# A cross-attention kernel: another order for the first five blocks, with division behind the values and seven-product matmuls from block 0

## The chip, the cores and the metric

The kernel runs on one core of one Trainium2 chip. The metric is the device time of one execution in microseconds (us), which is the time of that core. The core has five engines that matter here: TensorE (PE in the profile, its weight loads PEld), VectorE (DVE), ScalarE (ACT), GpSimd (POOL), and SyncE (SP), which here only issues DMAs. Each engine takes its own instructions in the order in which they were written; an instruction that must wait for another engine holds up everything behind it on its own engine. SBUF is the memory on the chip, PSUM the accumulator that TensorE writes to.

## What is computed

All in float32, with 16 batches of 1024 rows and 512 features, a context of 64 rows for each batch, and 16 heads of 32 features:

```python
def _ada_ln(x, c, W_ss, b_ss):
    h = (x - mu) / jnp.sqrt(var + EPS)          # mean and variance of each row
    scale, bias = jnp.split(jax.nn.silu(c) @ W_ss + b_ss, 2, axis=-1)
    return (1.0 + scale)[:, None, :] * h + bias[:, None, :]
xq = _ada_ln(x, cond, Wss_q, bss_q)
xkv = _ada_ln(ctx, cond, Wss_kv, bss_kv)
q = xq @ Wq + bq
k, v = split(xkv @ Wkv + bkv)
attn = softmax(q k^T / sqrt(32))                # for each head, over the 64 context rows
out = x + ((attn @ v) @ Wp + bp)
```

## The kernel before

**Tiling.** The 16384 rows are cut into 32 blocks of 512 (`i`; `NB` is 32, `TB` 512), two for each batch. Features are in four groups of 128 (`c`), rows of a block in four tiles of 128 (`t`), the 64 context rows in two halves of 32 (`z`). Keys and values are made for two batches at a time (`keys` or `key_products` with `key_tiles`, `value_products` with `value_tiles`).

**One block** goes through these steps, each a function:
- `load_x` (L139, SP) brings in 512 rows, 1 MB. `q_stats` (L296, VectorE) takes mean and variance of each row; `q_scale` (L305) makes the factors, in `rstd_of` (L263): with `apart` on ScalarE and POOL, without it on ScalarE and VectorE. `hidden` (L325, ScalarE) normalises.
- `turn` (L490, VectorE) transposes 32x32 pieces into `ht`; `move` (L502) puts them in their places in `xt` with 16 DMAs of 64 KB, all from SP. Features are then across partitions. (Block 0 is turned on TensorE instead.)
- The query projection has two forms. The plain form (`queries`, L533, with `queried` on ScalarE to copy out and add the bias) uses weights that were scaled for the batch (`query_weights`, L480) and 16 matmuls of 128x512 a block. The seven-product form (`query_product`, L607, with `query_out`, `query_added`, `query_seed`) multiplies halves and sums of halves by Strassen's scheme, 28 matmuls of 128x256 in place of 32 such; it needs `scale_features` (L562, ScalarE), `query_weight_sums` once and `feature_sums` (L593, both POOL).
- `scores` (L666) makes two PSUM pairs for each `z`; VectorE takes maxima out of them (`maximum`), ScalarE copies them to SBUF (`copied`). With `crossed` the two engines begin at different pairs, without it both begin at the first. `maxima` (L721) combines and spreads the maxima over the tile, `subtract` (L727, POOL unless told otherwise) takes them off, `weights` (L733, ScalarE) exponentiates.
- The division by the sum has two forms. Ahead of the values: `sums`, `inverse` and a `spread` on VectorE, then `divide` (L757, POOL) of both weight tiles, then `mix` (L809, TensorE) and `mixed` (ScalarE) to copy out. Behind the values: `total` (L765, POOL) adds the halves, `row_total` and `inverse_rows` (VectorE, five small DMAs through DRAM), `spread_rows`, and after `mix` the copy out is itself the division, `divided` (L800, VectorE).
- The output projection has two forms as well. Plain: `project` (L849), four times 4 matmuls of 128x512, with `projected`, which adds to the residual tile, on VectorE; `residual` (L330, POOL) has added the bias to that tile. Seven products: `biased` (ScalarE) seeds the PSUM bank with the bias, `row_sums` (L903, POOL) makes sums of halves, `product` (L915) multiplies, `added` (L942, VectorE) adds to the residual tile, seven times a block; `weight_sums` (L876, POOL) is done once.

**Order.** The order on every engine is written out by hand, as the sequence of calls at the end of the function: a way in for blocks 0 to 3, a regular loop from block 4 to 29 in which the steps of neighbouring blocks are interleaved, and a way out for the last two. Before, block 0 and 1 divide ahead of the values and are projected plainly, block 2 divides ahead of the values and is projected with seven products, and blocks 0 to 4 make their queries plainly. From block 3 on it divides behind the values, from block 5 on queries have seven products.

```python
        vb_tiles[i] = spread(i, v, f"vb_{i}", other=i in (1, NB - 1))
...
    mix(0, apart=False)
    mixed(0)
```

**Buffers.** A tile with the tag of an older one in a pool of one or two buffers waits until the older one is no longer read. `x` has two, `r` (residuals) two, `ht` one, `xt` two, `wq` two (also the sums of the query weights and features), `vb`, `qt`, `ot`, `s1` one each, `big0` to `big3` one each (first the scale and shift weights, later the score tiles: `i % 2 * 2 + z`). In PSUM, `ps_s` has two pairs of banks for scores and for `mix`, and four single banks go round in `ring`, of which two are left (`ring[:] = [0, 1]`) once banks 2 and 3 accumulate the seven products.

Of the kernel before, what the change touches and what calls it, by code (L numbers as in the profile page):

```python
# [20 lines left out]
def cross_attention_block(  # L21
# [16 lines left out]
):  # L38

# [99 lines left out]
    def load_x(i):  # L139
        t = xpool.tile([P, NT, H], F32, tag="x", name=f"x_{i}")  # L140
        nc.sync.dma_start(t, rows_of(x, i))
        x_tiles[i] = t
# [34 lines left out]
    for c in range(NC):  # L177
        nc.sync.dma_start(
            b_v_sb[c * 32 : (c + 1) * 32, :],
            b_kv[H + c * P : H + (c + 1) * P].rearrange("(o h) -> o h", o=1).to_broadcast([32, P]),  # L180
        )
# [123 lines left out]
    def q_scale(i, kvb=None):  # L305
        n = NT if kvb is None else NT + 1
        q_rstd[i] = rstd_of(q_mv.pop(i)[:, :n, :], n, "q", i > 1)
        if kvb is not None:
            kv_rstd[kvb] = (q_rstd[i], NT)
# [170 lines left out]
    def query_weights(b):  # L480
        t = qpool.tile([P, NC, H], F32, tag="wq", name=f"wq_{b}")
        for c in range(NC):
            scale = ss["q"][:, c, b : b + 1]
            if b == 0 and c % 2:
                nc.vector.tensor_scalar_mul(t[:, c, :], w_q_sb[:, c, :], scale)
            else:
                nc.scalar.mul(t[:, c, :], w_q_sb[:, c, :], scale)
        wq_tiles[b] = t

    def turn(i, ts):  # L490

        if ts[0] == 0:
            ht_tiles[i] = hpool.tile([P, 4, NC, NT, 32], F32, tag="ht", name=f"ht_{i}")
        for t in ts:
            nc.vector.transpose(
                ht_tiles[i][:, :, :, t, :].rearrange("p k c b -> p c k b"),
                x_tiles[i][:, t, :].rearrange("p (c k b) -> p c k b", c=NC, k=4),
            )
        if ts[-1] == NT - 1:
            x_tiles.pop(i)  # L500

    def move(i):  # L502
# [3 lines left out]
        for k in range(4):  # L506
            for g in range(4):
                nc.sync.dma_start(  # L508
# [24 lines left out]
    def queries(i, o, later=False):  # L533
        xt, b = xt_tiles[i], i // BPB
        w = wq_tiles.get(b, w_q_sb)
        if o == 0:

            tag = "vb" if i in (1, 3) else "qt"
            qt_tiles[i] = qpool.tile([P, NC, TB], F32, tag=tag, name=f"qt_{i}", bufs=1)
# [13 lines left out]
    def queried(i, o):  # L553
        pq, b = pq_tiles.pop((i, o)), i // BPB
        dst = qt_tiles[i][:, o, :]
# [194 lines left out]
    def inverse(i):  # L750

        v = small.tile([P, HPC * NJ], F32, tag="v", name=f"v_{i}")
        both(v, l_tiles.pop(i), ALU.add)
        nc.vector.reciprocal(v, v)
        vb_tiles[i] = spread(i, v, f"vb_{i}", other=i in (1, NB - 1))
# [9 lines left out]
    def total(i):  # L765

        t = big.tile([P, HPC, TB], F32, tag=f"big{(i + 1) % 2 * 2}", name=f"sum_{i}")
# [3 lines left out]
    def row_total(i):  # L771
# [7 lines left out]
        )  # L779

# [187 lines left out]
    query_bias_rows()  # L968
    kv_stats(0)
# [10 lines left out]
    load_x(2)  # L980
    load_residual(0)
    load_projection_bias()
# [3 lines left out]
    move(1)  # L986
    load_projection()
    load_x(3)
# [8 lines left out]
    hidden(2, range(NT))  # L997


    scores(0, 0)  # L1000
    turn(2, range(NT))
    move(2)
    load_context(2)
    load_x(4)
    load_residual(1)
    residual(0)
    value_products(0)
    scores(0, 1)
    maxima(0)
    subtract(0, nc.vector, (0,))  # L1010
    value_tiles(0)
    subtract(0, nc.vector, (1,))
    queries(1, 0)
    query_weights(1)
    queries(1, 1)
    weights(0, 0)
    queries(1, 2)
    weights(0, 1)
    sums(0, 0)
    queries(1, 3)  # L1020
    query_weight_sums()
    sums(0, 1)
    inverse(0)
    divide(0)
    scores(1, 0)
    queries(2, 0)
    q_stats(3)
    queries(2, 1)
    q_scale(3)
    scores(1, 1)  # L1030
    maxima(1)
    subtract(1)
    queries(2, 2)
    hidden(3, (0, 1))
    mix(0, apart=False)
    mixed(0)
    hidden(3, (2, 3))
    queries(2, 3)
    turn(3, range(NT))
    move(3)  # L1040
    kv_stats(2)
    q_stats(4)
    project(0, 0)
    weights(1, 0)
    sums(1, 0)
    project(0, 1)
    weights(1, 1)
    residual(1)


    load_x(5)
    q_scale(4)
    kv_scale(2)
    scores(2, 0)
    sums(1, 1)
    inverse(1)
    divide(1)
    project(0, 2)
    context_hidden(2)
    hidden(4, (0, 1))  # L1060
    scores(2, 1)
    maxima(2)
    subtract(2)
    weight_sums()
    hidden(4, (2, 3))
    project(0, 3)
    queries(3, 0)
    queries(3, 1)
    queries(3, 2)
    turn(4, range(NT))  # L1070
    load_residual(2)
    move(4)
    mix(1)
    mixed(1)
    q_stats(5)
    weights(2, 0)
    queries(3, 3)
    project(1, 0)
    sums(2, 0)
    weights(2, 1)  # L1080
    project(1, 1)
    sums(2, 1)
    inverse(2)
    divide(2)
    q_scale(5)
    context_features(2)
    scale_features(4)
    project(1, 2)


    load_x(6)
    scores(3, 0, crossed=True)
    project(1, 3)
    ring[:] = [0, 1]
# [3 lines left out]
    queries(4, 0)  # L1098
    load_residual(3)
    hidden(5, (0, 1))  # L1100
    biased(2, 2)
    mix(2)
    mixed(2)
    hidden(5, (2, 3))
    q_stats(6)
    turn(5, range(NT))
    move(5)
    q_scale(6)
    row_sums(2, 0)
    load_x(7)  # L1110
    queries(4, 1)
# [3 lines left out]
    weights(3, 0)  # L1115
    added(2, 2)
    biased(2, 3)
    weights(3, 1)
    total(3)
    queries(4, 2)  # L1120
    keys(2)
    hidden(6, range(NT))
    scale_features(5)
    row_sums(2, 1)
    turn(6, range(NT))
    load_x(8)
    product(2, 7)
    q_stats(7)
    value_products(2)
    value_tiles(2)  # L1130
    row_total(3)
    inverse_rows(3)
    queries(4, 3)
    feature_sums(5)
# [199 lines left out]
```

## Time and profile before

| | us |
|---|---|
| median of 3 runs | 1058.74 (1057.19 to 1059.29) |
| the profiled execution | 1058.86 |
| its span, first to last instruction | 1057.1 |
| POOL busy with divide (L760), mean of one | 4.52 |
| POOL `subtract` (L729), mean of one of 58 | 4.56 |
| POOL `total` (L768), mean of one | 4.54 |
| VectorE `divided` (L805), mean of one of two a block | 1.22 |
| VectorE `row_total` (L773), mean of one | 2.28 |
| mean granted TensorE clock | 0.998 |

The profile is of one execution. A row of a group gives line, engine, operation, output and inputs by the program's names, their shapes, the count, then the busy time of all and the mean of one in ns, and the idle time of the engine just before them with what ended it. A row of the timeline gives start and length in us, engine, line, operation, and in brackets the idle time ahead of it. TensorE's rows are pipelined: the distance between starts, not the length, is what a stage costs. A row of the table by stretch gives the stretch, its length, then the busy time of PE, PEld, DVE, ACT and POOL with counts, the granted clock, the DMA share and GB/s.

In the way in, the first scores begin at 39.7 us, the scores of blocks 1, 2, 3 at 60.7, 89.6 and 125.9, those of block 4, with which the loop begins, at 162.0, and those of block 5 at 197.0.

### The profile page before, as it was taken

Reading aid. Unit: us, or ns where it says so; the run is one execution under the profiler, and the core shown is the slowest. Engines: PE = TensorE matmul, PEld = TensorE weight load, DVE = VectorE, ACT = ScalarE, POOL = GpSimd, SP = SyncE. Lnnn points to the kernel's source line nnn. Section 1 sums busy time; section 2 is a strip of 40 time slices with the busy share of each in tenths; the row PEclk is TensorE's granted clock in tenths of the full one; section 3 lists DMA queues with packets and bytes.
Section 4 is the critical chain, followed back from the end, with each engine's and each line's share of the span. In section 5 each row is a group of like instructions: output and inputs, shape, how many; then the busy total and the mean of one; then the engine's idle time right before and its main releaser. Section 6 shows DMA issues by size and latency. Waiting matters only on the chain.

```text
span 1057.1 us, 22537 instructions
## 1 busy us (share of the span) xinstructions
PE 1033.6 (98%) x8914; PEld 733.7 (69%) x8914; DVE 854.7 (81%) x1134; ACT 618.0 (58%) x951; POOL 752.7 (71%) x470
## 2 busy tenths in 40 slices
PE   6999998999999999999999999999999999999998
PEld 4534365777777787777787787777777777777433
DVE  5698648987789877888878878898778887776993
ACT  3566665665575655667556666566566765565330
POOL 0258794889768869788668986688886886787340
PEclk9999999999999999999999999999999999999999
DMA  9743444444535344544345443444454443334202
GB/s 337 248 127 111 130 122 127 155 150 147 161 94 162 123 140 145 171 148 127 106 131 164 153 158 112 126 141 150 139 157 134 152 134 116 98 115 162 82 30 90
DMA packets 99976, 147.27 MB, mean 139 GB/s; under 512 B 29944, under 2 KB 30096, under 8 KB 99872
## 3 DMA queue, kind: packets, MB, share of 16 engines
q1 hardware_dynamic: 99872, 145.85, 43.5%
q8 instruction: 70, 1.15, 0.5%
q14 instruction: 34, 0.28, 0.1%
HBM read 78.85 MB, written 34.44 MB: 107 GB/s over the span
## 4 chain that ended last, share of the span: by engine, by line
PE 80%; DVE 5%; POOL 5%; DMA 4%; SPq 2%; issue 2%; ACT 1%; POOLq 0%; DVEq 0%; ACTq 0%
PE pp L933 28%; PE pq L625 27%; PE po L825 6%; PE ps L673 6%; PE pp L852 5%; PE pq L542 3%; SPq L508 2%; PE pv L431 2%; PE pk L395 2%; POOL s L760 2%; DMA wss_kv<-in_L_xcond_Wss_kv_dram 2%; DMA b_p_sb<-in_L_xcond_bp_dram 1%; POOL s L729 1%; DMA x<-in_x_dram 1%; DVE s L729 1%
## 5 line engine op out<-in xcount | busy, mean ns | idle before, releaser
L729 POOL TENSOR_TENSOR s<-s,mb 128x2048 f32<-128x2048 f32 x58 | 263.1, 4560 | 160.8 <-DVE mb L716 160.8
L694 ACT COPY s<-ps 128x1024 f32<-128x1024 f32 x128 | 129.5, 1012 | 119.7 <-DVE m L685 82.9
L685 DVE TRANSPOSE_TENSOR_REDUCE m<-ps 128x32 f32<-128x1024 f32 x128 | 150.6, 1214 | 27.1 <-PE ps L673 27.1
L655 ACT ACTIVATE qt<-pq,bias_t 128x256 f32<-128x256 f32 x208 | 85.8, 463 | 110.9 <-PE pq L625 110.9
L933 PE MATMUL pp<-w_p_sb,ot 128*128 128x256 f32 x648 | 148.7, 379 | 0.0
L735 ACT ACTIVATE s<-s 128x2048 f32<-128x2048 f32 x64 | 122.3, 1911 | 42.4 <-POOL s L729 31.8
L947 DVE TENSOR_TENSOR r<-pp,r 128x512 f32<-128x512 f32 x189 | 122.5, 670 | 25.5 <-PE pp L933 19.8
L933 PEld LDWEIGHTS pp<-w_p_sb,ot 128*128 128x128 f32 x648 | 123.4, 190 | 17.4 <-issue 0.7
L768 POOL TENSOR_TENSOR sum<-s,s 128x2048 f32<-128x2048 f32 x27 | 122.7, 4543 | 0.8 <-ACT s L735 0.8
L933 PEld LDWEIGHTS pp<-WT,s 128*128 128x128 f32 x432 | 78.9, 192 | 54.0 <-issue 29.3
L933 PE MATMUL pp<-WT,s 128*128 128x256 f32 x432 | 109.3, 397 | 0.0
L933 PE MATMUL pp<-WT,ot 128*128 128x256 f32 x432 | 102.2, 380 | 0.0
L625 PE MATMUL pq<-xt_sums,wq_sums 128*128 128x256 f32 x416 | 101.0, 386 | 0.0
L321 ACT ACTIVATE x<-x,rstdq 128x512 f32<-128x512 f32 x128 | 96.7, 807 | 4.8 <-POOL rstdq L285 3.2
L625 PE MATMUL pq<-xt,wq_sums 128*128 128x256 f32 x416 | 99.0, 381 | 0.0
L625 PEld LDWEIGHTS pq<-xt_sums,wq_sums 128*128 128x128 f32 x416 | 77.0, 190 | 31.1 <-issue 21.8
L625 PE MATMUL pq<-xt,w_q_sb 128*128 128x256 f32 x416 | 98.4, 380 | 0.1
L260 DVE BATCH_NORM_STATS2 bs<-x 128x6 f32<-128x512 f32 x128 | 86.9, 679 | 5.0 <-DMA x<-in_x_dram 5.0
L662 DVE TENSOR_TENSOR qt<-pq,qt 128x256 f32<-128x256 f32 x104 | 39.1, 418 | 63.1 <-PE pq L625 62.5
L933 PEld LDWEIGHTS pp<-WT,ot 128*128 128x128 f32 x432 | 82.2, 190 | 11.0
L565 ACT ACTIVATE xt<-xt,ss_q 128x512 f32<-128x512 f32 x112 | 84.7, 810 | 6.1 <-DMA xt<-ht 4.3
L625 PEld LDWEIGHTS pq<-xt,w_q_sb 128*128 128x128 f32 x416 | 79.1, 190 | 11.0 <-PE pp L933 0.4
(139 smaller groups left out, 1725.0 us busy)
## 6 DMA issues: line engine op xcount, KB each, us to landing
x<-in_x_dram SPq DMA_DIRECT2D x32, 1024.0 KB, 6.4
r<-in_x_dram SPq DMA_DIRECT2D x32, 1024.0 KB, 5.5
xt<-ht SPq DMA_DIRECT2D x496, 64.0 KB, 2.0
out_dram<-r SPq DMA_DIRECT2D x54, 512.0 KB, 3.8
out_dram<-r SPq DMA_DIRECT2D x20, 256.0 KB, 2.0
wss_q<-in_L_xcond_Wss_q_dram SPq DMA_DIRECT2D x2, 1024.0 KB, 8.8
ctx<-in_ctx_dram SPq DMA_DIRECT2D x8, 256.0 KB, 3.2
wss_kv<-in_L_xcond_Wss_kv_dram SPq DMA_DIRECT2D x2, 1024.0 KB
```

The lines of the kernel that those rows point to most:

```text
L260: nc.vector.bn_stats(bs, r)
L321: nc.scalar.activation(dst, src, AF.Identity, bias=rstd[:, 1, j : j + 1], scale=rstd[:, 0, j : j + 1])
L565: nc.scalar.activation(xt[:, :, c, :], xt[:, :, c, :], AF.Identity, scale=ss["q"][:, c, b : b + 1], bias=ss["q"][:, NC + c, b : b + 1],)
L625: nc.tensor.matmul(qa[k][:, m * HT : (m + 1) * HT].rearrange("p (g n) -> p g n", g=2), lhsT=a[:, c, m * P : (m + 1) * P], rhs=x[:, :, c, : ...
L655: nc.scalar.activation(dst, src, AF.Identity, bias=bq_t[:, o : o + 1])
L685: nc.vector.tensor_reduce(m_tiles[i][:, z, 2 * e : 2 * e + 2, :], pss[e].rearrange("p r (j a) -> p r j a", a=32), AX.X, ALU.max, apply_tra ...
L694: nc.scalar.copy(s_sb[:, 2 * e : 2 * e + 2, :], pss[e])
L729: eng.tensor_tensor(s_tiles[i, z], s_tiles[i, z], mb_tiles[i], ALU.subtract)
L735: nc.scalar.activation(p, p, AF.Exp, scale=SCALE)
L768: nc.gpsimd.tensor_tensor(t, s_tiles[i, 0], s_tiles[i, 1], ALU.add)
L933: nc.tensor.matmul(acc[k][:, t * HO : (t + 1) * HO], lhsT=rows[:, c, t * P : (t + 1) * P], rhs=cols[:, c, :], start=n == 2 and t == 0 and ...
L947: nc.vector.tensor_add(r, acc[k].rearrange("p (t h) -> p t h", t=2), r)
```

## The change

The way in is written anew; loop and way out are the same. In words:
- blocks 0, 1 and 2 divide behind the values and are projected with seven products; block 4 makes its queries with seven products. `residual`, `inverse`, `divide`, `mixed` and `project` are gone from the way in. Block 1 gets its sums from two `sums` and the new `halves_total` on VectorE, blocks 0 and 2 from `total` on POOL;
- in `move`, for blocks 1, 2, 3 and 5, every second group of four DMAs is issued by POOL (8 of 16);
- the scaled weights of batch 1 are made by POOL in one instruction, not by ScalarE in four;
- `q_scale(2)` is done without `apart`;
- other places: x_3 in a buffer of `r`, `ht` of block 2 in `big2`, the sum of block 0 in `ot`, the queries of block 3 in `qt`, and a query tile is only taken when the first copy into it is written;
- `load_x(2)` ahead of the value bias, the residual and projection-bias loads later; statistics, turns, copies, exponentials and POOL's sums in another order.

```diff
-        t = xpool.tile([P, NT, H], F32, tag="x", name=f"x_{i}")
+        t = xpool.tile([P, NT, H], F32, tag="r" if i == 3 else "x", name=f"x_{i}")
...
-        q_rstd[i] = rstd_of(q_mv.pop(i)[:, :n, :], n, "q", i > 1)
+        q_rstd[i] = rstd_of(q_mv.pop(i)[:, :n, :], n, "q", i > 2)
...
+        if b:
+            scale = ss["q"][:, :NC, b : b + 1].to_broadcast([P, NC, H])
+            nc.gpsimd.tensor_tensor(t, w_q_sb, scale, ALU.mult)
...
-            ht_tiles[i] = hpool.tile([P, 4, NC, NT, 32], F32, tag="ht", name=f"ht_{i}")
+            pool, tag = (big, "big2") if i == 2 else (hpool, "ht")
+            ht_tiles[i] = pool.tile([P, 4, NC, NT, 32], F32, tag=tag, name=f"ht_{i}")
...
-                nc.sync.dma_start(
+                (nc.gpsimd if i in (1, 2, 3, 5) and k % 2 else nc.sync).dma_start(
...
+            tag = "vb" if i == 1 else "qt"
+            qt_tiles[i] = qpool.tile([P, NC, TB], F32, tag=tag, name=f"qt_{i}", bufs=1)
...
+        if i == 0:
+            t = opool.tile([P, HPC, TB], F32, tag="ot", name="sum_0")
...
+    def halves_total(i):
+        lt_tiles[i] = small.tile([P, HPC, NJ], F32, tag="lt", name=f"lt_{i}")
+        both(lt_tiles[i].rearrange("p r j -> p (r j)"), l_tiles.pop(i), ALU.add)
```

The new order from the keys of block 0 to the loop, the loads of the residuals left out, a line for each stretch:

```python
keys(0); hidden(2, range(NT)); turn(2, range(NT)); move(2); query_weights(1); load_x(4); value_products(0); value_tiles(0)
scores(0, 0, crossed=True); q_stats(3); queries(1, 0); q_scale(3); scores(0, 1); maxima(0); subtract(0, nc.vector)
queries(1, 1); hidden(3, range(NT)); weight_sums(); queries(1, 2); weights(0, 0); turn(3, range(NT)); queries(1, 3); weights(0, 1); total(0); move(3)
scores(1, 0, crossed=True); queries(2, 0); row_total(0); inverse_rows(0); load_x(5); scores(1, 1); maxima(1); subtract(1)
queries(2, 1); queries(2, 2); biased(0, 2); mix(0); spread_rows(0); divided(0); queries(2, 3); weights(1, 0); queries(3, 0, later=True)
row_sums(0, 0); q_stats(4, (0, 1)); sums(1, 0); q_stats(4, (2, 3), kvb=2); weights(1, 1); product(0, 1); added(0, 1); product(0, 2); row_sums(0, 1); q_scale(4, kvb=2); query_weight_sums()
scores(2, 0, crossed=True); added(0, 2); biased(0, 3); queries(3, 1, later=True); scores(2, 1); queried(3, 0); queried(3, 1); hidden(4, range(NT)); maxima(2); subtract(2)
product(0, 7); added(0, 7); product(0, 6); added(0, 6); queries(3, 2); sums(1, 1); halves_total(1); inverse_rows(1); product(0, 5); added(0, 5); turn(4, range(NT)); move(4); load_x(6)
product(0, 4); added(0, 4); product(0, 3); added(0, 3); weights(2, 0); biased(1, 2); weights(2, 1); total(2); mix(1); spread_rows(1); divided(1); context_hidden(2); queries(3, 3)
q_stats(5); q_scale(5); row_sums(1, 0); context_features(2); product(1, 1); added(1, 1); product(1, 2); added(1, 2); row_sums(1, 1); biased(1, 3); row_total(2); inverse_rows(2); scale_features(4)
scores(3, 0, crossed=True); feature_sums(4); product(1, 7); product(1, 6); added(1, 7); added(1, 6); scores(3, 1); maxima(3); subtract(3); query_product(4, 1); query_seed(4); hidden(5, (0, 1, 2))
product(1, 5); added(1, 5); query_product(4, 2); query_out(4, 2); product(1, 4); product(1, 3); hidden(5, (3,)); spread_rows(2); q_stats(6, (0, 1)); added(1, 4); added(1, 3); biased(2, 2)
mix(2); q_stats(6, (2, 3)); divided(2); turn(5, range(NT)); load_x(7); q_scale(6); row_sums(2, 0); move(5); query_product(4, 6); weights(3, 0); query_out(4, 6); product(2, 1); added(2, 1); product(2, 2); added(2, 2); weights(3, 1); total(3)
query_product(4, 7); query_out(4, 7); biased(2, 3); row_sums(2, 1); key_products(2, spare("pk_2")); hidden(6, range(NT)); query_product(4, 5); query_added(4, 5); key_tiles(2); query_product(4, 4); query_added(4, 4); row_total(3); inverse_rows(3)
scale_features(5); turn(6, range(NT)); load_x(8); value_products(2, spare("pv_2")); value_tiles(2); query_product(4, 3); query_out(4, 3); feature_sums(5); product(2, 7); q_stats(7); move(6); q_scale(7)
```

## The prediction, made before the changed kernel was seen

> **What bounds the kernel now.** I read the page's engine shares first, then the busy time by stretch, then TensorE's timeline, then the other queues around each wait.
>
> ```profile
> PE 1033.6 (98%) x8914; PEld 733.7 (69%) x8914; DVE 854.7 (81%) x1134; ACT 618.0 (58%) x951; POOL 752.7 (71%) x470
> ```
>
> TensorE is the bound nearly everywhere, so an edit pays by taking matmuls away or by taking a wait of TensorE away. Where are waits left?
>
> ```profile
> 39.69:161.96 122.27, 119.22 (x957) 55.35 (x957) 89.13 (x109) 77.38 (x115) 88.06 (x55) 1.00 0.45 137
> 161.96:196.98 35.02, 32.01 (x241) 23.55 (x241) 31.36 (x47) 20.82 (x35) 23.17 (x15) 0.95 0.51 160
> 196.98:226.61 29.63, 29.63 (x246) 22.74 (x245) 26.64 (x36) 19.77 (x32) 24.48 (x16) 1.00 0.45 143
> ```
>
> The rows are the way in (from the first scores to those of block 4), the first pass of the regular loop, and its second; the columns are length, then busy PE, PEld, DVE, ACT, POOL, clock, DMA. The second pass has no idle TensorE; its 29.63 us hold 0.43 us of context turns, so a plain pass is 29.2. The first takes 35.02. The timeline says why, and prices the two forms of product:
>
> ```profile
> 60.72 2.16 PE L673 MATMUL ps<-qt,kt 32*32 32x512 f32 x32
> 82.60 7.03 PE L852 MATMUL pp<-w_p_sb,ot 128*128 128x512 f32 x16
> 98.87 10.46 PE L542 MATMUL pq<-xt,wq 128*128 128x512 f32 x24
> 142.27 3.62 PE L933 MATMUL pp<-w_p_sb,ot 128*128 128x256 f32 x16
> 170.84 1.25 PE L673 MATMUL ps<-qt,kt 32*32 32x512 f32 x32 [2.94 <-ACT s L694]
> ```
>
> A half of the scores spans 1.14 us when nothing holds it; the first line has 2.16, so busy rows hide waits too. From start to start, a plain projection or query piece takes 3.47 us (10.40/3, 6.96/2), one of seven products 1.73 (3.45/2), half the scores 1.07, a mix 2.28, keys 3.57, values 3.63. The last line is a wait of 2.94 us; right behind it the granted clock is halved, and one product takes 3.4 us instead of 1.73:
>
> ```profile
> 172.00:173.00 1.00, 1.00 (x9) 0.84 (x3) 1.00 (x2) 0.00 (x0) 0.00 (x0) 0.50 0.17 17
> 174.00:175.00 1.00, 1.00 (x4) 0.82 (x3) 0.42 (x1) 0.88 (x2) 0.00 (x0) 0.50 0.36 88
> ```
>
> So a wait near 3 us costs 1.7 us more than its length.
>
> **The sum before**, from the end of keys(0) at 38.9 to scores(5,0) at 196.98, 158.1 us: scores 10 x 1.07 = 10.7; values and keys 3.63 + 7.6; queries 1 to 4, 16 x 3.47 = 55.5; four mixes 9.1; plain projections of 0 and 1, 8 x 3.47 = 27.8; 17 products 29.4. That is 143.7, so 14.4 us are waiting or half clock.
>
> **Matmuls removed.** Projections 0 and 1 go from 27.8 to 14 x 1.73 = 24.2 (-3.6); queries of block 4 from 13.9 to 7 x 1.73 = 12.1 (-1.8). Together -5.4, all on the path, because TensorE is the bound.
>
> **The other engines.** POOL loses divide(0 to 2) (six of 4.52, 27.1) and residual(0), (1) (10.0); it gains total(0), (2) (9.1), row sums of 0 and 1 (8 x 1.28 = 10.2), feature_sums(4) (5.1), query_weights(1) (nearest row 4.54) and 32 DMA issues. VectorE loses, per block divided earlier, two row sums and a spread, and gains row_total or a half, spread_rows and divided (2.3 each); its seven `added` are 4.7 against four of 0.65. ScalarE loses `mixed` (about 2 a block) and query_weights(1) (2.55), and gains `biased` (two of 0.59 a block). All of this lies beside TensorE; only order decides what it costs. scale_shift, the loop from pass 5 and the way out do not change. Values(0) ahead of scores(0,0) fill the 0.78 us wait for `kt`.
>
> **Loads moved.** x_2 is issued ahead of the value bias, but it stands behind the same weights and landed at 33.9; before the engines use it, TensorE has work to 38.7: nothing. r_0 and b_p no longer stand ahead of move(1) on SP; with half its DMAs on POOL, xt_1 is there well before 43.5, where before it came at 46.5 (wait 0.97). x_3 has a buffer of its own; behind 8 issues it lands near 45, when q_stats(3) wants it.
>
> **Buffers and small steps.** turn(2) stood until 46.49 for move(1) to release its buffer (3.22 us of VectorE); in `big2`, free since the scale rows, it ends at 42.4. q_scale(2) goes from POOL to four VectorE operations of 0.17 us, while TensorE is at queries(0,3) and keys(0) to 38.7; without that cover it would cost 0.8. sum_0 in `ot`, and qt_3 in `qt`, wait for readers that are done in the walk below (scores(2,1) the latest); if not, queries(3,0) would hold its bank and TensorE with it. On SP, load_residual(2) and (3) stand until `added` has sent out the old tile (3.8 us to land); behind them wait inverse_rows(2) and load_x(7), both wanted over 5 us later: nothing.
>
> **POOL's DMA issues** are not in this trace. The nearest rows are SP's:
>
> ```profile
> 31.20 13.44 SPq L508 DMA_DIRECT2D xt<-ht  x16
> 145.86 10.02 SPq L508 DMA_DIRECT2D xt<-ht  x16
> ```
>
> 10.02/16 = 0.63 us each (the first was held up by loads). The Trainium skill speaks against the move: "DMA: Bandwidth & Descriptors", section "Issuing engines are not separate DMA queues", says that another issuing engine saves only the sequencer's issue time; section "Latency and other measured facts" gives about 1 us to the first byte for POOL against 0.6 for SP. But issue time is what SP's row is made of. By the row, eight cost POOL 5.0 us; by the page's ratio (an estimate) 8.4. Below: 0.3 us each, POOL would only be earlier. I take the row, 0.6.
>
> **A walk through the queues** (each engine's order in the diff, durations from the rows): scores(0,0) at 42.4, queries(1,0) to 47.0, scores(0,1) to 48.0, queries(1,1 to 3) to 58.4. Scores(1,0) need the last query copy. On ScalarE that copy stands behind hidden(3) and weights(0,0). hidden(3) waits for rstd(3) on POOL, behind move(2) (42.4 + 4.8 = 47.2) and query_weights(1) (51.8): 52.9. Behind hidden(3) on ScalarE stand queried(1,2) and the exponentials; it ends at 55.9.
>
> weights(0,0) wait for subtract(0), now on VectorE beside weight_sums on POOL. Here is a price:
>
> ```profile
> L729 DVE TENSOR_TENSOR s<-s,mb x6: 2278/2288/5518, 54.0 to 1019.1; 128x2048 f32<-128x2048 f32 x6
> ```
>
> Alone it takes 2.28 us; beside POOL's divide at the end it took 5.52. The skill's "SBUF — State Buffer", section "Who interferes with whom", says that a VectorE instruction with two SBUF inputs and a reading POOL instruction exclude each other: the second waits for the first's end. POOL's pieces here are 1.27 long, so I let them alternate; by the 2.28 row alone, subtract(0) would end at 59.6, by the rule at 61.4. I take 61.4. Then the query copy ends at 60.4: **wait 1 = 2.0**, wait 2 (scores(1,1) behind turn(3)'s maxima) **1.3**.
>
> total(0) ends at 68.0; row_total, reciprocal and DMAs (4.7, as 168.6 to 173.3 before) bring the divisors at 75.6, when VectorE is through maxima(1). divided(0) ends at 80.5, product(0,1) starts at 83.6: no wait. To mix(1) at 105 TensorE runs. Behind divided(1) VectorE does q_stats(5), to 115.0; ScalarE's rstd(5) and POOL's q_scale(5) stand ahead of row_sums(1,0), which end at 119.8, while TensorE is done with scores(3,0) at 115.9: **wait 3 = 4.0**, and half clock and the copies of scores(3,0), behind context_features(2) and scale_features(4) on ScalarE, hold scores(3,1) to 125: **1.7**. product(2,1) waits for divided(2): **1.0**. Scores(4,0) start at 159.3 (before 161.96). POOL's half of move(5) is ahead of total(3), so row_total(3), turn(6), values and q_stats(7) end at 162.4, some 2 us behind the scores, where before they were 5.5 behind: **1.5** in the first pass. Waits left: 11.5, and 1.3 of seams between stages.
>
> Scores(5,0) then start at 38.9 + 138.3 + 12.8 = 190.0, not 196.98: 7.0 us less. VectorE's slack in the loop (26.64 busy of 29.63) wipes out the remaining lag.
>
> The profiled execution took 1058.86 (span 1057.1 and 1.8 around it), the median of the runs is 1058.74. 1058.86 - 7.0 = 1051.9; I say **1052**.
>
> **Rivals.** *Fewer waits (0.2):* DVE runs earlier than I have it and wait 3 with its half clock (5.7) does not come, perhaps wait 1 (2.0) neither: 1052 - 5 to 8 = 1044 to 1047. For it: VectorE is 89.1 of 122.3 in the way in, ScalarE 77.4, so no engine is full. Against: order, not volume, makes my waits.
>
> *Waits only move (0.18):* two more waits of 1 to 2 us on the crowded ScalarE queue, one reaching the half clock (1.7): 1055.5 to 1060.5, say 1057. For it: only 5.4 us are certain, and each of the walk's queues has a wait for a third engine ahead of somebody's copy.
>
> *POOL becomes the bound, slower (0.12):* each of POOL's DMAs costs over 1 us. move(2) then pushes rstd(3), hidden(3) and scores(1,0) by 8 us for each further us per DMA; above about 1.0, move(3), which stands ahead of subtract(1), pushes that one too (slack 75.9 - 72.8 = 3.1), 16 us for each us together. At 1.05 the gain is 7.0 - 1.9 = 5.1; at 1.4 nothing is left; at 2.0 the time is about 1068. For it: POOL is 88.1 busy of 122.3 and gets 32 issues that were SP's. Against: before, SP needs 0.63.
>
> That seven products do not replace the plain form can be excluded: loop and block 2 run them at 1.73 already.
>
> **How the numbers follow.** The forecast case, 1048 to 1055.5, has 0.5; fewer waits 0.2; waits only move 0.18; slower 0.12. A measurement here tells about 0.2% (2.1 us) from no change, that is faster below 1056.6 and slower above 1060.9. Faster: 0.5 + 0.2 + 0.06 = 0.76; same 0.12; slower 0.12. The range leaves out the lower third of the second case and most of the last: 1045 to 1059.
>
> **What would show it.** Right: the plain projection's count (L852, 160 here) falls by 64, queries (L542, 192) by 32; scores(4,0) begin near 159, scores(5,0) near 190; a wait on POOL's row sums ahead of product(1,7), and a slice with half clock behind it. Wrong: POOL's gaps between turn(2) and query_weights(1) over 8 us; subtract(0) at 2.28 us each; TensorE without a wait from 60 to 125 (then 1046); or a wait in a pass after scores(5,0), where I count none.

## The result, and the profile after

| | us |
|---|---|
| after, median of 14 runs | 1056.42 (1053.91 to 1059.10) |
| before, median of 14 runs beside them | 1058.08 (1056.26 to 1060.44) |
| ratio, 95% interval | 0.9986 [0.9975, 0.9996] |
| the profiled execution, its span | 1058.46, 1056.2 |

The change saves 1.7 us, 0.14%, where the forecast was 1052 and so 6 to 7. The time lies inside the range of 1045 to 1059, in the case that the prediction called "waits only move".

First the engine shares of the page, then the busy time by stretch. The stretches end at the same scores as those of before (first of block 4, of block 5, of block 6); the first one starts at the same 39.69 us, where after has the values of block 0 and only at 43.32 its first scores:

```profile
PE 1028.8 (97%) x8986; PEld 747.5 (71%) x8986; DVE 863.7 (82%) x1150; ACT 611.0 (58%) x940; POOL 762.7 (72%) x495
```

```profile
39.69:166.20 126.51, 116.88 (x1030) 70.89 (x1029) 102.51 (x126) 70.82 (x106) 97.06 (x78) 0.97 0.47 140
166.20:196.98 30.78, 29.65 (x242) 22.51 (x241) 27.61 (x43) 19.85 (x34) 20.57 (x13) 1.00 0.61 181
196.98:226.61 29.63, 29.63 (x246) 22.70 (x246) 26.65 (x36) 19.78 (x32) 24.75 (x16) 1.00 0.47 145
```

TensorE has 4.8 us less to do (1033.6 to 1028.8), nearly what the removed matmuls are worth, and the first pass of the loop went from 35.02 to 30.78, as forecast (30.7). But the way in is 4.2 us longer, not 2.7 shorter, and its clock is 0.97, not 1.00. Scores(5,0) begin at 196.98, to the hundredth where they began before. So the matmuls were saved, and given back before 166.20. TensorE's timeline shows where:

```profile
120.14 1.99 PE L949 MATMUL pp<-WT,ot 128*128 128x256 f32 x8 [3.22 <-POOL ot L925]
...
134.98 2.35 PE L841 MATMUL po<-s,vt 32*32 32x512 f32 x64
137.25 1.99 PE L633 MATMUL pq<-xt_sums,wq_sums 128*128 128x256 f32 x8
143.77 6.46 PE L949 MATMUL pp<-w_p_sb,ot 128*128 128x256 f32 x16 [4.52 <-ACT workq L284]
150.07 1.89 PE L633 MATMUL pq<-xt_sums,wq_sums 128*128 128x256 f32 x8
```

The wait of 3.22 ahead of product(1,7) is the forecast's wait 3. The wait of 4.52 ahead of product(2,1) (forecast: 1.0) is the new one. Behind it two products take 6.30 us from start to start, where two took 3.5: TensorE is at half clock, as the stretch shows (the column behind the five engines is the clock):

```profile
143.80:150.10 6.30, 6.30 (x17) 5.08 (x18) 4.04 (x6) 4.20 (x4) 5.82 (x12) 0.56 0.69 226
```

The row puts the wait down to ScalarE's `workq` (L284), which ended at 143.68. But product(2,1) doesn't read it: it multiplies what divided(2) has scaled on VectorE, whose first half was done at 143.62. And `workq` itself is made from q_stats(6), which stand in VectorE's queue too. So VectorE's queue has to be read:

```profile
118.98 0.55 DVE L800 RECIPROCAL lt<-lt 128x64 f32<-128x64 f32 x1
...
130.60 0.65 DVE L963 TENSOR_TENSOR r<-pp,r 128x512 f32<-128x512 f32 x1
135.82 2.31 DVE L811 STREAM_TRANSPOSE vb<-vr 128x2048 f32<-128x2048 f32 x1 [4.56 <-DMA vr<-ltd]
...
142.42 2.33 DVE L821 TENSOR_TENSOR ot<-po,vb 128x1024 f32<-128x1024 f32 x2
```

spread_rows(2) (L811) waits 4.56 us for its divisors from DRAM, and behind it stand statistics, two `added` and divided(2) (L821). Why were the divisors late? Their reciprocal (L800) was done at 119.5. SP's queue, which sends them off (`ltd` is the way out to DRAM, `vr` the four ways back):

```profile
106.59 10.95 SPq L516 DMA_DIRECT2D xt<-ht  x16
117.64 0.52 SPq L143 DMA_DIRECT2D x<-in_x_dram  x1
118.26 0.99 SPq L965 DMA_DIRECT2D out_dram<-r  x2
126.99 0.38 SPq L150 DMA_DIRECT2D r<-in_x_dram  x1
127.46 0.46 SPq L803 DMA_DIRECT2D ltd<-lt  x1
132.77 1.75 SPq L805 DMA_DIRECT2D vr<-ltd  x4
```

load_residual(2) (L150; it stands behind added(0,3), among the loads that the order above leaves out) may write its buffer only when the output of block 0 has left it. That output was issued from 118.26 on, and its second half took 8.1 us to land, behind x_6; until then SP stood. The divisors' 32 KB then went out behind the load's 1 MB and took 5.29 us to land. The chain of waits has the same in one view:

```profile
118.83 8.08 DMA out_dram<-r
...
126.99 0.38 SPq L150
...
127.46 5.29 DMA ltd<-lt
```

And the output itself left late because move(4), all on SP, held the queue from 106.59 to 117.54 with its 16 issues.

### The profile page after: what moved, and what is told of

The parts are those of the page before. It is cut to its first block, busy times and chain, and to the rows that moved or that the text cites. A ratio compares the mean times of both kernels' runs of the same rounds, so it can differ in the third digit from the quotient of the medians.

```text
span 1056.2 us, 22776 instructions
## 1 busy us (share of the span) xinstructions
PE 1028.8 (97%) x8986; PEld 747.5 (71%) x8986; DVE 863.7 (82%) x1150; ACT 611.0 (58%) x940; POOL 762.7 (72%) x495
## 4 chain that ended last, share of the span: by engine, by line
PE 86%; DVE 7%; DMA 2%; issue 1%; ACT 1%; POOL 1%; SPq 0%; DVEq 0%; POOLq 0%
PE pp L949 31%; PE pq L633 30%; PE po L841 6%; PE ps L681 6%; PE pq L546 4%; PE pp L868 3%; PE pk L398 3%; PE pv L434 2%; DVE m L693 1%; DVE bs L263 1%; DVE s L737 1%; DMA out_dram<-r 1%; DMA ltd<-lt 1%; DVE lt L785 1%; POOL s L737 1%
## 5 line engine op out<-in xcount | busy, mean ns | idle before, releaser
L693 DVE TRANSPOSE_TENSOR_REDUCE m<-ps 128x32 f32<-128x1024 f32 x128 | 150.8, 1215 | 30.7 <-PE ps L681 26.9
L949 PE MATMUL pp<-w_p_sb,ot 128*128 128x256 f32 x696 | 162.5, 384 | 4.5 <-ACT workq L284 4.5
L963 DVE TENSOR_TENSOR r<-pp,r 128x512 f32<-128x512 f32 x203 | 131.6, 670 | 26.9 <-PE pp L949 19.4
L949 PEld LDWEIGHTS pp<-w_p_sb,ot 128*128 128x128 f32 x696 | 134.0, 193 | 24.4 <-ACT workq L284 4.9
L780 POOL TENSOR_TENSOR sum<-s,s 128x2048 f32<-128x2048 f32 x29 | 131.7, 4543 | 3.5 <-ACT s L743 3.5
L949 PEld LDWEIGHTS pp<-WT,s 128*128 128x128 f32 x464 | 83.7, 189 | 54.9 <-issue 29.8
L949 PE MATMUL pp<-WT,s 128*128 128x256 f32 x464 | 115.2, 391 | 0.0
L949 PE MATMUL pp<-WT,ot 128*128 128x256 f32 x464 | 109.8, 379 | 3.2 <-POOL ot L925 3.2
L633 PE MATMUL pq<-xt_sums,wq_sums 128*128 128x256 f32 x432 | 104.9, 386 | 0.0
L949 PEld LDWEIGHTS pp<-WT,ot 128*128 128x128 f32 x464 | 88.0, 190 | 16.9 <-POOL ot L925 4.1
L633 PEld LDWEIGHTS pq<-xt,wq_sums 128*128 128x128 f32 x432 | 80.5, 190 | 11.5 <-issue 1.4
```

Source lines behind the costliest of these rows:

```text
L633: nc.tensor.matmul(qa[k][:, m * HT : (m + 1) * HT].rearrange("p (g n) -> p g n", g=2), lhsT=a[:, c, m * P : (m + 1) * P], rhs=x[:, :, c, : ...
L693: nc.vector.tensor_reduce(m_tiles[i][:, z, 2 * e : 2 * e + 2, :], pss[e].rearrange("p r (j a) -> p r j a", a=32), AX.X, ALU.max, apply_tra ...
L780: nc.gpsimd.tensor_tensor(t, s_tiles[i, 0], s_tiles[i, 1], ALU.add)
L949: nc.tensor.matmul(acc[k][:, t * HO : (t + 1) * HO], lhsT=rows[:, c, t * P : (t + 1) * P], rhs=cols[:, c, :], start=n == 2 and t == 0 and ...
L963: nc.vector.tensor_add(r, acc[k].rearrange("p (t h) -> p t h", t=2), r)
```

## Experiments

The theory to be tested: the missing gain is this chain, a load that stands at the head of SP's queue with the divisors behind it, plus the half clock that the wait brings on. Two rivals: the divisors are late because of traffic, and would be so in any order; or something else in the new order eats the gain, GpSimd's DMA issues or VectorE beside GpSimd. (The letters A and B in an expectation are its own.) Edits are to the kernel after. Ratios are to the kernel before on the same chip, with 95% intervals.

### The load of the residual behind the divisors

```diff
     added(0, 3)
-    load_residual(2)
...
     inverse_rows(2)
+    load_residual(2)
```

> The changed kernel with one load moved: the residual of block 2 is issued behind the small DMAs that bring the divisors of block 2, not ahead of them. Theory (the divisors of block 2 stand on SP behind a load that waits for an output to land, and then share the rings with it): the 7.9 us that the first divisor DMA stands on SP and its landing of 5.3 us instead of 1.5 go; the spread of the divisors does not wait on VectorE (4.56 us now), TensorE waits at most 1 us ahead of the product behind divided(2) (4.5 now) and does not fall to half clock there; scores(4,0) start near 158.8 (166.2 now), and the time is about 7 us below the changed kernel: 1049 to 1050.5, ratio to before 0.991 to 0.993. Rival A (the small DMAs are slow because POOL's DMAs and the loads share the DMA engines, whatever the order on SP): landing stays at 5 us, gain 0 to 1.5 us. Rival B (the product waits for ScalarE's seed copy behind added, as the wait's last releaser says): no gain.

Measured: 1051.64 us (1050.18 to 1053.56), ratio 0.9941 [0.9928, 0.9954]. SP's queue and then TensorE's:

```profile
117.43 0.99 SPq L965 DMA_DIRECT2D out_dram<-r  x2
118.86 0.86 SPq L803 DMA_DIRECT2D ltd<-lt  x1
125.95 2.06 SPq L805 DMA_DIRECT2D vr<-ltd  x4
128.12 0.39 SPq L150 DMA_DIRECT2D r<-in_x_dram  x1
```

```profile
138.27 3.69 PE L949 MATMUL pp<-w_p_sb,ot 128*128 128x256 f32 x16
141.79 1.89 PE L633 MATMUL pq<-xt_sums,wq_sums 128*128 128x256 f32 x8
```

The divisors leave 8.6 us earlier and product(2,1) follows without a wait and at full clock. Scores(4,0) begin at 157.92 (after: 166.20; forecast: 159.3), scores(5,0) at 188.72 (forecast: 190.0). With one line moved, the forecast comes true; that the median fits it to 0.4 us is in part luck, as the profiled execution (1050.18) lies 1.7 below the walk's. A part of the traffic rival is true as well: `ltd` now took 7.1 us to land, behind x_6 and the output, so the divisors were there only 6.5 us earlier, at 129.2 (after: 135.7), 1.1 us before spread_rows(2) wanted them:

```profile
130.34 2.29 DVE L811 STREAM_TRANSPOSE vb<-vr 128x2048 f32<-128x2048 f32 x1
```

### The stand without the traffic

A small piece of the residual tile (32 bytes for each partition) is loaded where load_residual(2) was, so SP stands as long as before; the whole tile is loaded behind the divisors.

```diff
-    load_residual(2)
+    r_2 = xpool.tile([P, NT, H], F32, tag="r", name="r_2")
+    nc.sync.dma_start(r_2[:, 0:1, 0:8], rows_of(x, 2)[:, 0:1, 0:8])
...
     inverse_rows(2)
+    nc.sync.dma_start(r_2, rows_of(x, 2))
+    r_tiles[2] = r_2
```

> The changed kernel, in which the load of the residual of block 2 is cut in two: 32 bytes of 128 rows stay where the load was and wait as it did, the whole load follows behind the divisors' DMAs. So the stand on SP is kept and the traffic in front of the divisors is not. Theory (stand of 7.9 us and slow landing of 3.7 us together exceed a slack of 7 us, each alone hardly does): the first divisor DMA still starts near 127.4 but lands in 1.5 us, the spread on VectorE waits about 1 us, TensorE 1 to 2 us without half clock; 5 to 6.5 us below the changed kernel, 1050 to 1051.5. If the stand alone carries it: within 2 us of the changed kernel. If the traffic alone carries it: as the run with the load moved.

Measured: 1051.65 us (1050.00 to 1053.14), ratio 0.9937 [0.9925, 0.9949].

```profile
126.73 0.36 SPq L1101 DMA_DIRECT2D r<-in_x_dram  x1
127.18 0.38 SPq L803 DMA_DIRECT2D ltd<-lt  x1
128.70 2.29 SPq L805 DMA_DIRECT2D vr<-ltd  x4
131.03 0.43 SPq L1123 DMA_DIRECT2D r<-in_x_dram  x1
```

SP stood just as long (the piece left at 126.73), but `ltd` landed in 1.5 us, the divisors were there at 132.4, and spread_rows(2) did not wait:

```profile
133.51 2.29 DVE L811 STREAM_TRANSPOSE vb<-vr 128x2048 f32<-128x2048 f32 x1
```

This profile flatters the stand: half clock behind wait 3 (119.35 to 126.17 us) brought VectorE to spread_rows(2) at 133.5, where in after it was free at 131.3. Measured against that, the stand alone would leave a wait of about 1.1 us (an estimate from these rows), not 4.56. So neither half of the chain makes the loss: a stand of 8 us alone costs about 1 us or nothing, and a landing 5.6 us late alone nothing (the run before); only the two in a row cost more.

### The stand made shorter

Block 4's moves are shared by SP and GpSimd as those of blocks 1, 2, 3 and 5 are.

```diff
-                (nc.gpsimd if i in (1, 2, 3, 5) and k % 2 else nc.sync).dma_start(
+                (nc.gpsimd if i in (1, 2, 3, 4, 5) and k % 2 else nc.sync).dma_start(
```

> The changed kernel, in which the DMAs of move(4) too are issued half by POOL. Theory (the first cause is SP, which issues 16 DMAs of move(4) from 106.6 to 117.5, so that the output of block 0 leaves at 118.3 and the load behind it stands to 127): SP is free some 5 us earlier, the output leaves near 112, the load at 121, the divisors land by 131: no wait of the spread, 5.5 to 7 us below the changed kernel, 1049.5 to 1051. POOL's 4 us fall between subtract(2) and total(2), where row_total(2) has no slack of more than 2.6: up to 1 us back. Rival A (POOL's DMAs are what slows the small ones): worse than the changed kernel by 0.5 us or more.

Measured: 1050.59 us (1050.33 to 1050.94), ratio 0.9927 [0.9915, 0.9939]. The output leaves at 112.85, load_residual(2) at 121.90, the divisors' `ltd` at 122.37; it still lands late (4.9 us), but in time: product(2,1) waits 0.18. SP's rows, then TensorE's:

```profile
112.85 0.99 SPq L965 DMA_DIRECT2D out_dram<-r  x2
121.90 0.38 SPq L150 DMA_DIRECT2D r<-in_x_dram  x1
122.37 0.46 SPq L803 DMA_DIRECT2D ltd<-lt  x1
```

```profile
138.33 3.69 PE L949 MATMUL pp<-w_p_sb,ot 128*128 128x256 f32 x16 [0.18 <-ACT workq L284]
```

Three different edits take the chain apart in three places, all end within 1.1 us of each other, and all reach what was forecast. The second rival (something else in the new order) isn't needed for the missing gain.

### Without GpSimd's DMA issues

```diff
-                (nc.gpsimd if i in (1, 2, 3, 5) and k % 2 else nc.sync).dma_start(
+                nc.sync.dma_start(
```

> The changed kernel with all DMAs of all moves on SP, as before. POOL loses 4 times 4.0 us, SP gets 4 times 5 us. If [...]another issuing engine saves next to nothing: within 1 us of the changed kernel. From the trace: move(3) would hold SP from 64 to 74, and the divisors of block 0, wanted at 76.0, come at 79.5; block 1 and 2's queues as now; so 2 to 4 us above the changed kernel, 1058 to 1060.5. If POOL's issues hurt (16 us of POOL, and a slow path for small DMAs): below it.

Measured: 1063.06 us (1062.03 to 1065.86), ratio 1.0048 [1.0035, 1.0060]. Without this part the whole change is slower than the kernel before. SP's row of move(1), and TensorE's of scores(1,0):

```profile
32.70 10.46 SPq L516 DMA_DIRECT2D xt<-ht  x16
```

```profile
63.30 1.25 PE L681 MATMUL ps<-qt,kt 32*32 32x512 f32 x26 [1.54 <-ACT qt L568]
```

With all 16 issues on SP, move(1) runs from 32.70 to 43.16 (after: 8 issues, to 38.20), so x_3 is issued at 43.21 instead of 38.25, and the roots of its statistics on ScalarE, with hidden(3) and a query copy behind them, come 2.4 us later. Scores(1,0) then wait 1.54 us. Move(2) takes 14.72 us where its 8 took 8.77, and the lag grows to 6.2 us by scores(3,0) (121.98, after: 115.78); two stretches at half clock (64.19 to 67.61 and 98.33 to 101.74 us), which after doesn't have, are about half of it. The divisors of block 2 leave 5.0 us later and product(2,1) still waits 3.83. So sharing the issues is worth 6.6 us of the medians, with the chain of the residual load in both kernels, where I had expected 2 to 4. The Trainium skill, "DMA: Bandwidth & Descriptors", section "Issuing engines are not separate DMA queues", says that another engine saves only the issue time and calls that usually small beside the transfer. The first half fits; here that time is the larger part: each of a move's DMAs lands 2.0 us after its issue in the median of the execution, and the 16 issues of one of the first five moves take 10.35 to 14.72 us.

GpSimd's price, which the prediction had bounded without seeing it, is on the trace of after (the bracket is the idle time ahead of it):

```profile
32.34 4.13 POOL L516 DMA_DIRECT2D xt<-ht  x8 [31.02 <-DVE ss_kv L251]
```

0.52 us each here, 0.50 in the other three moves, so the slower rival (over 1 us each) was far off.

### What holds wait 3

Product(1,7) still waits 3.16 us in the first experiment. GpSimd's row sums are moved ahead of q_scale(5); then scale_features(4) behind the copies of scores(3,0) on ScalarE; then block 4's moves shared as well. Each kernel has the edits of the one before it, and load_residual(2) behind the divisors.

```diff
     divided(1)
+    row_sums(1, 0)
...
     q_scale(5)
-    row_sums(1, 0)
```

> The first experiment's order (load of residual tile 2 behind the divisors of block 2), and GpSimd's row sums of tile (1,0) directly behind the division of tile 1, ahead of q_scale(5). Theory A (wait 3 is decided by GpSimd's row sums): the 3.2 us wait of product (1,7) goes and the product starts near 116.6. But scores (3,1) stay near 123 us, because the copies behind scale_features(4) on ScalarE end last there: total gain at most 0.5 us on the first experiment's 1051.6, 1051.0 to 1051.7. Theory B (the row sums are the only limit): scores (3,1) at 120.2 and the total near 1048.4. Half clock after the wait should also not be seen any more.

```diff
-    scale_features(4)
     scores(3, 0, crossed=True)
+    scale_features(4)
```

> The kernel of the run before it, and scale_features(4) moved behind scores (3,0), so that ScalarE makes the copies first. Theory A: with both chains early, scores (3,1) start near 121.2 instead of 123.4; then the divisors of block 2, which land near 129.6, are wanted at 128.2 and cost a wait of about 1.4. Sum 1 to 2 us below the first experiment: 1049.5 to 1051.0. Theory B (one chain is enough): the same time as the run before.

The edit of the third kernel is that of the shorter stand above.

> The kernel of the run before it, and move(4)'s DMAs also shared between SP and GpSimd's queue, so that the output of block 0 leaves some 5 us earlier and the divisors land near 126. Theory A: the wait of 1.4 us for the divisors does not occur; scores (5,0) near 186.5, total 1048.0 to 1049.5, ratio 0.990 to 0.992. Theory B (GpSimd has no time for eight more issues of 0.5 us): GpSimd's row sums or q_scale(5) come 4 us later and the time is that of the run before or more, 1050 to 1053.

Measured: 1050.72, 0.9925 [0.9913, 0.9938]; 1050.22, 0.9918 [0.9905, 0.9932]; 1050.74, 0.9927 [0.9914, 0.9939]. The three don't differ, and are at most 1.4 us better than the first experiment (2.4 by the ratios), with intervals that overlap. The first went as its theory A had it at scores(3,1) (123.04), with a total 0.3 us below the range given, but not in its step: product(1,7) went only from 119.43 to 118.45.

```profile
118.45 1.97 PE L949 MATMUL pp<-WT,ot 128*128 128x256 f32 x8 [2.41 <-ACT pp L912]
```

The row sums were done at 115.7. Now biased(1,3) (L912) on ScalarE ends last; it stands behind the features of the context, and those behind the roots of q_stats(5). I had not seen this third chain. The second's total lies in the range of its theory A, but the step again failed; the third came out as theory B had it, with GpSimd's row sums 1.7 us later than in the second (done at 117.95, 116.23 there). In both, the copies that scores(3,1) wait for ended early (121.24 in the second; 122.99 in the first), but in both profiles half clock came behind the wait, and product(1,7) took 3.3 us or more from start to start. The second kernel's:

```profile
119.05 3.46 PE L949 MATMUL pp<-WT,ot 128*128 128x256 f32 x8 [2.47 <-ACT pp L912]
```

Scores(3,1) then began at 124.17 and 123.90, hardly earlier than in after (124.23).

### The weight sums later

The first experiment's order, with GpSimd's weight_sums() no longer beside subtract(0) on VectorE.

```diff
-    weight_sums()
...
     move(3)
+    weight_sums()
```

> The first experiment's order, and weight_sums() (GpSimd) moved behind move(3), so that it no longer lies beside subtract(0) on VectorE. Theory A (two-input work on GpSimd slows VectorE): subtract(0) takes 2 x 2.28 = 4.6 us instead of 6.42, the pieces of weight_sums 1.27 us instead of 3.32, and scores (1,0) and (1,1) come up to 1.3 us earlier; total 1050.3 to 1051.6. Theory B (the two lie side by side without effect on each other): subtract(0) still 6.4 and the total that of the first experiment or, since the sums then stand ahead of other work of GpSimd, up to 1 us more.

Measured: 1049.98 us (1048.45 to 1051.14), ratio 0.9921 [0.9908, 0.9935]. Two timelines of after, VectorE's and GpSimd's, show what this takes away:

```profile
55.18 6.42 DVE L737 TENSOR_TENSOR s<-s,mb 128x2048 f32<-128x2048 f32 x2
```

```profile
54.90 1.27 POOL L897 TENSOR_TENSOR WT<-w_p_sb 128x512 f32<-128x512 f32 x1
56.13 3.32 POOL L898 TENSOR_TENSOR WT<-w_p_sb,WT 128x512 f32<-128x512 f32 x1
59.41 2.79 POOL L899 TENSOR_TENSOR b_diff<-b_p_sb 128x256 f32<-128x256 f32 x1
```

And VectorE's in the experiment:

```profile
54.22 4.49 DVE L737 TENSOR_TENSOR s<-s,mb 128x2048 f32<-128x2048 f32 x2
```

The two instructions of subtract(0) take 4.49 us instead of 6.42, and GpSimd's pieces 1.29 and 0.75 instead of 3.32 and 2.79: while they lie side by side, both are slow. Scores(1,1) begin at 64.19 (first experiment: 65.58), and the 1.4 us stay to scores(5,0), 187.37 against 188.72. Of these, 0.34 were there before the edit could act (scores(0,0) at 42.36, 42.70 there), so the edit gives 1.0. That the effect is there is shown by the trace; of the total, the two intervals overlap, so it can't be told in the medians.

### The best order

The last kernel with block 4's moves shared; and the same with all three chains of wait 3 set free, biased(1,3) ahead of the context's features on ScalarE and these and scale_features(4) behind the copies of scores(3,0):

> The kernel with weight_sums() late (1049.98 in its own run), and move(4)'s DMAs shared between SP and GpSimd's queue. Theory A (the divisors of block 2 are no longer on the path, they land before spread_rows(2) wants them): the same time within 0.7 us, 1049.3 to 1050.7. Theory B (GpSimd's 8 more issues of 0.5 us push its row sums at wait 3): up to 4 us more, 1051 to 1054.

```diff
     divided(1)
+    row_sums(1, 0)
...
     q_stats(5)
-    q_scale(5)
-    row_sums(1, 0)
-    context_features(2)
...
     added(1, 2)
-    row_sums(1, 1)
     biased(1, 3)
+    q_scale(5)
+    row_sums(1, 1)
...
-    scale_features(4)
     scores(3, 0, crossed=True)
+    context_features(2)
+    scale_features(4)
```

> The kernel of the run before it, and all three things that were seen to hold wait 3 set free: GpSimd's row sums of tile (1,0) directly behind divided(1), biased(1,3) ahead of the K features of context block 2 on ScalarE, and those features and scale_features(4) behind the copies of scores (3,0). Theory A (wait 3 had three chains, each ending within 1.5 us of the others, so that freeing one or two gave under 1 us): product (1,7) follows scores (3,0) with under 0.5 us of wait, scores (3,1) start near 119.5 instead of 122.05, total 1047 to 1048.3. Theory B (something else holds it as well): 1049.3 to 1050.5. A chance that spread_rows(2) then waits 1 to 2 us for its divisors.

Measured: 1050.67 (1048.37 to 1051.20), 0.9932 [0.9920, 0.9944]; 1050.25 (1049.12 to 1051.44), 0.9933 [0.9921, 0.9945]. The first as its theory A had it; the second with the time of its theory B. TensorE's timeline of the second:

```profile
117.54 1.99 PE L949 MATMUL pp<-WT,ot 128*128 128x256 f32 x8 [1.47 <-POOL ot L925]
119.76 1.99 PE L949 MATMUL pp<-WT,s 128*128 128x256 f32 x8 [0.23 <-POOL s L928]
121.69 1.14 PE L681 MATMUL ps<-qt,kt 32*32 32x512 f32 x32
123.60 2.26 PE L633 MATMUL pq<-xt,w_q_sb 128*128 128x256 f32 x8 [0.78 <-ACT xt L573]
```

Wait 3 is down to 1.47, but GpSimd's eight issues of move(4) (106.36 to 110.36) now stand ahead of total(2) and the row sums, and scale_features(4), moved back, holds the next query product for 0.78; the value tiles cost another 0.46 at 158.6. Scores(5,0) begin at 189.51, 146.1 us behind scores(0,0), as in the first experiment (146.0). So every version with the chain broken ends at 1050 to 1051.7, a saving of 0.6 to 0.8%, and which of them is the best these runs can't tell.

## Why the prediction was wrong

**The failed step.** It is the sentence "On SP, load_residual(2) and (3) stand until `added` has sent out the old tile (3.8 us to land); behind them wait inverse_rows(2) and load_x(7), both wanted over 5 us later: nothing." The queue was named and what stands in it too, and "over 5 us later" was right: the divisors were ready at 119.5 and wanted at 131.3, and their way takes 4.7 us in the walk, which leaves 7. What was put at nothing came to 11.7, by three terms taken wrong. The output took 8.1 us to land, not 3.8, with x_6 sent off just ahead of it. It left late, at 118.26, because move(4)'s 16 issues, which stay on SP, stand ahead of load_x(6) and of it: that queue I did not walk. These two made the stand 7.9 us. And the divisors, once issued, took 5.29 us for their way out, not the median of 1.5, behind the load that had just been let go: 3.8 more. What 11.7 exceeds 7 by is the wait of 4.56. The 3.8 for the output was a median of the whole execution, and the divisors' way a row of a quieter place; here 3 MB (x_6, the output, the residual tile) were sent off within 10 us.

**What it cost**, by the stages of the walk, in the profiled executions (us; the first experiment is the change without this step):

| | walk | after | first experiment |
|---|---|---|---|
| scores(0,0) | 42.4 | 43.32 | 42.70 |
| scores(3,1) | 125 | 124.23 | 123.39 |
| scores(4,0) | 159.3 | 166.20 | 157.92 |
| scores(5,0) | 190.0 | 196.98 | 188.72 |

From scores(3,1) to scores(4,0) the walk has 34.3, the first experiment 34.5, the change 42.0: 7.4 us are this step, 4.5 to 4.7 of wait and 2.8 of half clock. The other stages come within 2 us. Of the medians the step is less, 4.8 us (1056.42 against 1051.64; by the ratios 0.45%): the profiled execution of the change is 2.0 above its own median, that of the experiment 1.5 below. Runs of the change lie 5.2 us apart, the first experiment's 3.4. A late landing and a half clock that come in some runs and not in others would make such a spread (whether half clock comes depends on where its grid lies in an execution, see the last section); no profile was taken of a short run of the change, so this stays open.

**Point by point.**
- *Matmuls removed, -5.4:* the rows agree, and the counts are as forecast: plain projections 96 (160 before), plain queries 160 (192). TensorE's busy time fell by 4.8, with more half clock in it after than before.
- *Waits 1 and 2 (2.0 and 1.3):* too large. Scores(1,0) started at 59.60 behind an undisturbed start of 43.32, with 0.2 us of wait inside, and scores(1,1) waited 0.57.
- *VectorE beside GpSimd:* taken by the rule at 61.4 for its end; it ended at 61.6, and the experiment gives 4.49 without the neighbour. Here the rule and not the 2.28 row was the right price.
- *Wait 3 (4.0) and behind it (1.7):* 3.22 and 0.5, without the half clock that was forecast; scores(3,1) at 124.23 instead of 125. It was put down to GpSimd's row sums; the experiments show that ScalarE's biased(1,3) and the copies end within 1.5 us of them, so that taking away GpSimd's share shortened the wait from 3.16 to 2.41 and no more.
- *GpSimd's issues:* 0.50 each, for 0.6 taken between 0.3 and 1.05: eight take 3.9 to 4.1 us, so that the estimate of 8.4 was twice too high. Landing needs no price of its own: the profile's medians, 5.3 us for GpSimd's and 2.0 for SP's, are of different times. Within the same move the two land alike (SP's 3.1, 8.5, 2.0, 7.0 us in moves 1, 2, 3, 5; GpSimd's 3.7, 8.1, 2.0, 8.3).
- *First pass (1.5 above a plain one):* 1.6 (30.78 against 29.2).
- *Rivals:* "waits only move" is nearest in time (1057), with one wait of 4.5 us and the half clock instead of two on ScalarE. It was given 0.18; its reason, that each queue has a wait for a third engine ahead of somebody's copy, was right, but looked for on ScalarE when it was on SP.

## What to carry to other kernels

When loads, stores and a small round trip through DRAM share one queue, walk that queue like an engine's: a load that waits for its buffer to be sent out holds every transfer behind it, and the small one, once free, stands behind the load's megabyte. A median landing is no price for a transfer next to 1 or 2 MB of others; take the longest one seen beside such traffic, and put the small, wanted transfer ahead of the large, unwanted one. And before a wait is credited to the releaser that the profile names, look for the next chain: here three ended within 1.5 us, and freeing one gave only the distance to the second.

## What was not expected of the hardware

**Half clock comes on a grid of 3.41 us; what counts is how much of a wait falls into one stretch of it.** Waits of TensorE between 100 and 155 us, with the product behind them: half clock (3.3 to 3.6 us for one product) after 2.34, 2.47, 2.70, 3.02 us, and after 3.83 and 4.52; full clock (1.8) after 2.41, 3.00, 3.02, 3.08, 3.16, 3.22. So the wait's length doesn't decide, and kernels that differ up to the wait near 120 us in one load alone (the change and the first two experiments) got either. The granted clock shows what does. In each of the twelve traces it changes only at whole multiples of 3.413 us from its first entry (with all issues on SP at 64.19, 98.33, 125.64 and 149.53: 10, 8 and 7 such steps apart), and the grid lies elsewhere in each trace. Three stretches of this grid in after, then in the kernel with both chains freed (the first number behind the length is TensorE's busy time, 1.00 or 0.50 the clock):

```profile
115.25:118.66 3.41, 1.67 (x35) 0.42 (x33) 3.31 (x4) 3.25 (x13) 1.93 (x5) 1.00 0.42 102
118.66:122.08 3.42, 1.94 (x9) 1.74 (x10) 1.94 (x3) 3.32 (x6) 3.26 (x4) 1.00 0.89 195
122.08:125.49 3.41, 3.04 (x41) 1.59 (x39) 2.19 (x3) 2.10 (x3) 3.25 (x4) 1.00 1.02 369
```

```profile
115.26:118.67 3.41, 1.32 (x34) 0.23 (x32) 3.27 (x4) 3.38 (x13) 3.08 (x7) 1.00 0.63 100
118.67:122.09 3.42, 3.04 (x7) 2.50 (x8) 2.65 (x3) 3.03 (x5) 1.13 (x1) 0.50 0.79 249
122.09:125.50 3.41, 3.41 (x43) 2.02 (x42) 1.52 (x3) 1.98 (x3) 1.28 (x1) 1.00 0.94 354
```

In after the edge at 118.66 cuts the wait of 3.22 us in two, and the clock stays; in the other 2.1 of the 2.47 us lie in one stretch, and the next has half clock. From 30 to 1040 us in the twelve traces, each of the seven stretches at full clock with TensorE busy for 1.32 us or less was followed by half clock; of those with 1.63 or more only two were, both with all issues on SP (1.87 and 1.97 us), and what sets these apart stays open. Half clock lasted one stretch, or two where TensorE stood for 0.8 or 1.2 us of the first: hence 2.8 us in after, and 1.7 in the case before that the prediction's rule ("a wait near 3 us costs 1.7 us more") was made from. The Trainium skill, "TensorE: Matmul & The Clock Gate", section "Part 1: The HAM clock gate (the "warmup" mystery)", has a window of about 3.4 us that doesn't start with the kernel's work, and an idle window as what throttles. The grid fits that window; but a wholly idle one isn't needed, since five stretches with TensorE busy for 0.9 to 1.3 us were enough, and here the rows decide.

**Small transfers behind large ones.** The same 32 KB to DRAM (`ltd`) took 1.5 us to land in the second experiment, 4.9, 5.29 and 6.0 behind a residual load, 7.1 behind an x load and an output, though each was issued as soon as SP came to it.
